# Loads in half-megabyte pieces with two under way, in an expert layer and an attention layer on one core

## The chip, the core and the metric

The kernel runs on one core of a Trainium2 chip. TensorE (PE in the profile) multiplies matrices, VectorE (DVE), ScalarE (ACT) and GpSimd (POOL) work on tiles, and SyncE (SP) issues nearly all transfers. Each engine works through its own list of instructions in order and waits on semaphores for the others. The metric is the time of the device for one execution, in microseconds (us); lower is better.

## The reference

An input of 8 sequences of 512 rows and 256 columns goes through two layers, all in float32. In the first, each sequence picks one of 8 experts by an index; in the second, attention with 16 heads adds a bias that is read from memory for every head, query and key (8 x 16 x 512 x 512 numbers, 134 MB).

```python
def _L0_cond_ref(input_tensor, expert_idx, Wi, bi, Wo, bo, gamma, beta):
    Wi_b = Wi[expert_idx]
    ...
    h = jax.nn.gelu(jnp.einsum('bsh,bhi->bsi', input_tensor, Wi_b) + bi_b[:, None, :], approximate=False)
    o = jnp.einsum('bsi,bih->bsh', h, Wo_b) + bo_b[:, None, :]
    r = o + input_tensor
    ...
    return y * g_b[:, None, :] + be_b[:, None, :]

def _L1_cond_ref(src, src_mask, timestep, attention_bias, W_ada, b_ada, ...):
    emb = jax.nn.silu(_sin_emb(timestep)) @ W_ada + b_ada
    scale, shift = jnp.split(emb[:, None, :], 2, axis=-1)
    x = _ln(src) * (1.0 + scale) + shift
    ...
    scores = jnp.einsum('bhqd,bhkd->bhqk', q / math.sqrt(HEAD_DIM), k)
    scores = scores + attention_bias
    scores = jnp.where(src_mask, -jnp.inf, scores.astype(jnp.float32))
    probs = jax.nn.softmax(scores, axis=-1).astype(v.dtype)
    ctx = jnp.einsum('bhqk,bhkd->bhqd', probs, v)
    ...
    x = x + (ctx @ Wo + bo)
    h = _ln(x) * g2 + beta2
    ff = _gelu2(h @ W1 + b1) @ W2 + b2
    return x + ff
```

## The kernel before, in words

The kernel works through the 8 sequences, called batches here. For each there are an expert layer (`expert_layer`), projections to queries, keys and values (`projections`, `values`), 16 attention steps (`attention_step`, 128 in all, `s` counts them) and a feed-forward layer (`feed_forward`; for the last batch `feed_forward_part`).

*The planner.* None of this is issued in the order in which it is written. Each piece of work is an `op` of the class `Weave`: an engine, a cost in microseconds, a key, the ops that it waits for, the buffers it takes and uses, and a function that emits the instructions. `Weave.run` goes through a modelled time and always emits the op that can start first; among ops that can start within 0.25 us of each other, it takes the one with the lowest key. The keys are in units of attention steps. They come from tables: `PLACES` gives each layer of each batch a start and an end on that scale, `DUE` and `LAST_DUE` shift the parts of an attention step, and `AHEAD` says by how much a load is put ahead of its first user (the last lines of the function). So a change of a table or of a modelled cost gives all five engines another order, with the same work.

*Loads.* `load` makes an op of SP with a cost of the megabytes divided by 0.26. Nearly all loads go by SP's one queue: the bias (`fs`, 1 MB a step, L1085), the masks (`m`, four loads of 32 KB for two steps, L1092), the expert and feed-forward weights (`w`, 1 MB each, L428, L434, L490), the input (`xn`, L422) and its transposed copy (`xt`, L425), 0.5 MB each, the rows of biases and norms (`rows`, L462), and `br`, the first bias of an expert (L439). The outputs leave by it too (L915). As SP is in order, a load that waits for its buffer holds back everything behind it. Every load also has one of eight semaphores in turn, and waits until the one eight before it has landed.

*Buffers.* The bias has five pairs of tiles for two steps each; four steps share two pairs and give them back when the sums over their probabilities are done (L1211). There are two weight buffers, of 1 MB each, one for `rising` and one for `falling` in turn.

*The start.* The index of the experts is loaded by SP (L359), made safe by five small DVE instructions (L368 to L374) and read into a register of SP (`at_expert`, L405). Then `br` of batch 0, its `xt`, another index register and `br` of batch 1, and the first weights in four pieces of 256 KB. On PE the first instruction is the transposition of `br` (L742), and the first weights follow (`up`, L654, then `down`, L677).

*Attention.* Scores begin with a matmul that adds the mask (L1115) and go on with queries times keys (L1122); DVE adds the bias in place and keeps the row maximum (L1135); POOL negates the maximum (L1148); ACT takes the exponential (L1156); DVE transposes (L1171); four steps together are multiplied with the values (L1211), which are 4096 small matmuls of 64x32 in all, and divided. PE runs in three ways of using its array: "dense" 128x128, "scores" 32x64 and "sums" 64x32.

Float32 matmuls run as two passes, so PE has about 27,800 instruction words (weight loads, matmuls and waits). They are fetched from memory while the kernel runs, by the queue that the profile calls q8.

The change touches `load`, the emitting functions of the loads, `expert_layer`, and the tables.

Of the kernel before, what the change touches and what calls it, by code (L numbers as in the profile page):

```python
# [30 lines left out]
def _constants():  # L31
# [13 lines left out]
    for i in range(TURN_PIECES):  # L45
# [13 lines left out]
    "up": [  # L59
        (-30.99, -29.18, 11.93), (-23.38, -4.64, 1.67), (-2.2, -2.19, 2.72), (8.9, 18.36, 0.44),  # L60
        (36.48, 42.61, 6.68), (52.4, 66.61, 8.22), (74.01, 74.43, 3.8), (94.6, 84.17, 0.61),
    ],
    "down": [
        (-28.55, -10.44, -3.1), (3.09, -1.08, -3.11), (8.81, 10.29, 4.11), (14.74, 25.12, -3.62),
        (45.17, 45.46, 12.91), (65.74, 66.53, 0.58), (76.48, 85.13, 4.33), (100.77, 101.12, 0.3),
    ],
    "norm": [
        (-20.56, -11.71, -7.89), (11.44, 22.43, 14.05), (12.2, 41.92, -0.32),
        (21.3, -1.88, -4.88), (15.78, -6.61, -23.47), (31.45, 83.45, -37.13), (93.6, 53.91, -1.4),
        (95.74, 57.42, -8.52),  # L70
    ],
    "project": [
        (-9.61, -7.68, -11.33), (7.41, 20.72, -7.24), (30.64, 30.31, 8.68), (37.76, 54.11, 8.55),
        (49.54, 49.16, 2.1), (80.07, 77.16, 8.86), (97.75, 101.79, 9.6), (104.12, 108.8, -7.13),
    ],
    "values": [
        (0.47, 9.52, 8.56), (20.68, 19.13, 7.24), (38.76, 39.17, 6.29), (52.2, 50.21, -1.61),
        (73.42, 60.72, 3.32), (86.58, 92.54, 11.08), (95.65, 103.53, -1.95),
        (106.56, 111.1, -0.7),
    ],  # L80
    "last_norm": [
        (19.55, 40.44, 3.34), (45.17, 39.05, 0.73), (61.79, 44.12, -1.46), (69.83, 74.12, -1.04),
        (77.81, 88.16, -7.35), (111.66, 102.86, 5.55), (117.29, 111.01, -0.55),
    ],
    "last_up": [
        (30.73, 23.09, -4.57), (46.9, 42.38, 0.97), (68.15, 61.42, 5.34), (86.06, 77.08, 0.85),
        (95.3, 97.21, -3.28), (106.19, 120.06, 3.39), (125.24, 116.66, -2.08),
    ],
    "last_down": [
        (38.56, 21.97, -2.41), (50.89, 52.01, -2.88), (77.89, 66.69, 10.77),  # L90
        (86.82, 82.51, -9.57), (100.48, 114.32, 9.19), (122.04, 112.91, 5.18),
        (124.61, 130.66, 3.47),
    ],
    "last_part": [
        (129.58, 149.24, 3.32), (145.88, 182.54, 3.18), (154.27, 187.28, -2.8),
    ],
}

DUE = {
    "load_m": -0.49, "load_f": 1.05, "convert": -3.58, "add": 1.67, "neg": 0.82, "exp": 0.61,  # L100
    "turn": 5.48, "rec": 9.91, "diagonal": 11.03, "sums0": 2.58, "sums1": 8.57, "sums2": 9.88,
    "sums3": 9.26, "own": 9.45, "spread": 3.43, "divide": 9.16, "out": 6.89, "out_add": 11.41,
}
LAST_DUE = {
    "exp": 1.14, "turn": 8.27, "neg": 6.94, "rec": 7.94, "diagonal": 7.04, "sums0": 2.02,
    "sums1": 5.67, "sums2": 16.43, "sums3": 15.43, "own": 16.77, "spread": 10.61, "divide": 15.33,
    "out": 14.39, "out_add": 30.01,
}

PUT_BACK = {  # L110
    "table": 2.33, "tiles": 0.43,
}

AHEAD = {
    "xt": 2.56, "wi": 1.92, "br": 19.29, "x": -5.59, "wo": 3.7, "row": -0.14, "w1": -3.8,
    "w2": 0.69, "ss": 10.41,
}
# [145 lines left out]
def tile_expert_ffn_then_conditioned_layer(  # L263
# [94 lines left out]
    idx_in = const([1, B], "idx_in", I32)  # L358
    nc.sync.dma_start(idx_in, expert.unsqueeze(0))  # L359
    n_c = 3 + TURN_PIECES  # L360
# [24 lines left out]


    def load(mb, key, emit, **kw):
        return op("SP", mb / 0.26, key, emit, lands=1.8, **kw)

# [29 lines left out]
    for b in range(B):  # L419

        def x_in(b=b):
            nc.sync.dma_start(xn[b].tile, x[b].rearrange("(t p) d -> p t d", p=P))  # L422

        def xt_in(b=b):
            nc.sync.dma_start(xt_h[b].tile, x_t[b])  # L425

        def wi_in(b=b, of=slice(0, FF)):
            nc.sync.dma_start(  # L428
                rising(wi[b])[:, :, of],
                e_wi[at_expert(b)].rearrange("o (c p) f -> p (o c) f", p=P)[:, :, of],  # L430
            )

        def wo_in(b=b):
            nc.sync.dma_start(  # L434
                falling(wo_e[b]), e_wo[at_expert(b)].rearrange("o (c p) d -> p (o c) d", p=P)
            )

        def br_in(b=b):
            nc.sync.dma_start(br[b].tile, e_bi[at_expert(b)].rearrange("o (c p) -> (o c) p", p=P))  # L439

        ld_xt[b] = load_first(b, 0.5, -40, "xt", xt_in, takes=[xt_h[b]])
        if b:
            ld_wi[b] = [load_ahead(1.0, "wi", wi_in, takes=[wi[b]])] * NF
        else:

            ld_wi[b] = []
            for n in range(0, NF, 2):
                def piece_in(n=n, wi_in=wi_in):
                    wi_in(of=slice(n * P, (n + 2) * P))

                o = load(
                    0.25, -39 + 0.01 * n, piece_in, takes=[] if n else [wi[b]],
                    uses=[wi[b]] if n else [],
                )
                ld_wi[b] += [o, o]
        ld_br[b] = load_first(b, 0.02, -39.5, "br", br_in, takes=[br[b]])
        ld_x[b] = load_first(b, 0.5, -37.5, "x", x_in, takes=[xn[b]])
        ld_wo[b] = load_first(b, 1.0, -37, "wo", wo_in, takes=[wo_e[b]])
        ld_rows[b] = []
        for i, v in enumerate((e_bo, e_gamma, e_beta)):  # L460
            def row_in(b=b, i=i, v=v):
                nc.sync.dma_start(  # L462
                    rows[b][i].tile,
                    v[at_expert(b)].rearrange("o d -> (o d)").partition_broadcast(P),
                )

            ld_rows[b].append(load_first(b, 0.3, -36, "row", row_in, takes=[rows[b][i]]))
# [20 lines left out]

    def chunks_in(dst, src):
        return lambda: nc.sync.dma_start(dst, src.rearrange("(c p) n -> p c n", p=P))  # L490

# [25 lines left out]
    for b in range(B):  # L517
        ld_w1[b] = load_ahead(
            1.0, "w1", lambda b=b: chunks_in(rising(w1_h[b]), w1)(), takes=[w1_h[b]]
        )  # L520
        ld_w2[b] = load_ahead(
            1.0, "w2", lambda b=b: chunks_in(falling(w2_h[b]), w2)(), takes=[w2_h[b]]
        )
# [211 lines left out]
    def expert_layer(b):  # L735
# [12 lines left out]
        )  # L748
        first.append((0.2, [(a, 0.0), (e, -1.0)]))
        bias = pool_rows(  # L750
# [3 lines left out]
        def make(f, h, a):  # L754
# [4 lines left out]
                ),  # L759
                deps=[a], uses=[h, bc[b], hid], table="gelu",  # L760
            )

        hids = up(first, lambda: rising(wi[b]), (ld_wi[b], wi[b]), xt, [ld_xt[b], e], hid, make)
        mv = s_mv.new()
# [307 lines left out]
    def attention_step(s):  # L1072
# [11 lines left out]
        def load_f():  # L1084
            nc.sync.dma_start(f(), fside[b, i].rearrange("h q u k -> (h q) u k"))  # L1085

# [201 lines left out]
    for o, what in ahead:  # L1288
        o.key = min(a.key for a in o.after) - AHEAD[what]
    w.run()  # L1290
# [56 lines left out]
```

## Time and profile before

| | |
|---|---|
| runs | 933.25, 933.5, 937.66 us; median 933.5 |
| profiled execution | 933.9 us |
| its span, first to last instruction | 932.1 us |
| granted TensorE clock | 1.000 |
| moved by DMA | 198.08 MB, mean 213 GB/s (191.73 MB read from HBM) |
| first matmul of L654 | at 10.99 us |
| last matmul starts | at 928.4 us |

The time of a run is a little over the span; the span is what the profile divides up. A row of waits gives engine, line, what it waited for, the total in us, the number of times and the longest. A row of the timeline gives start and length in us, engine, line and operation, the output and inputs by the program's names, how many instructions it merges and, in brackets, the idle time before it with what ended it. "SPq" rows are issues of transfers: the time is that of the issue, not of the transfer. The table of DMA issues has, for one transfer from issue to landing, medians of 5.9 us for 1 MB of bias, 3.5 for 0.5 MB of `xt`, 3.3 for 256 KB of `ss` and 3.6 for 32 KB of mask. The trace also holds each packet of each DMA queue with its start, length and size; where the text speaks of packets, they are from there.

### The profile page before, as it was taken

To read this page: it belongs to the slowest core of one execution; us is meant where nothing else is said; L and a number is where in the kernel's file an instruction comes from. 1 tells how busy PE (TensorE), PEld (TensorE's weight loads), DVE (VectorE), ACT (ScalarE), POOL (GpSimd) and SP (SyncE) were. 2 spreads that over 40 slices of the span, in tenths; PEclk is the share of its full clock that TensorE was granted. 3 is DMA by queue.
4 is the path that set the end of the run, shared out by engine and by line. 5 is a ranking of instruction groups with operands and counts; after the bars stand their busy time and mean duration, and the time that the engine had idled before them with its cause. 6 is when DMAs were issued, how large, how long until landed. Compare 5 with 4: busy or idle time off the path is not lost.

```text
span 932.1 us, 33095 instructions
## 1 busy us (share of the span) xinstructions
PE 904.5 (97%) x13841; PEld 531.7 (57%) x13841; DVE 774.7 (83%) x1837; ACT 677.1 (73%) x1452; POOL 297.8 (32%) x380
## 2 busy tenths in 40 slices
PE   5999999999999999999999999999999999999998
PEld 2655564654564574655556546656465555564687
DVE  1226999989999999889999979879889999898951
ACT  2336768758859969589978797595876977959753
POOL 1171636124511435132225322133512632122210
PEclk9999999999999999999999999999999999999999
DMA  7378655676567676557666556754765466567410
GB/s 227 110 245 297 218 207 185 210 253 211 210 225 245 226 280 254 204 208 254 256 223 221 170 195 250 267 191 149 274 240 195 180 249 237 201 228 266 155 59 24
DMA packets 77596, 198.08 MB, mean 213 GB/s; under 512 B 8484, under 2 KB 54902, under 8 KB 61062
## 3 DMA queue, kind: packets, MB, share of 16 engines
q1 hardware_dynamic: 77158, 195.93, 59.3%
q8 instruction: 108, 1.77, 0.8%
q14 instruction: 42, 0.34, 0.1%
q10 hardware_dynamic: 288, 0.04, 0.0%
HBM read 191.73 MB, written 4.21 MB: 210 GB/s over the span
## 4 chain that ended last, share of the span: by engine, by line
PE 66%; DVE 2%; ACT 2%; issue 1%; POOL 0%; DMA 0%; ACTq 0%; DVEq 0%
PE d L677 17%; PE d L654 14%; PE d L1211 11%; PE sc L1122 8%; PE d L825 4%; PE sc L1115 4%; PE d L1254 2%; PE d L873 2%; PE d L1027 2%; PE d L632 1%; PE d L1227 1%; DVE fs L1135 1%; ACT fs L1156 1%; DVE fs L1171 0%; ACT L948 0%
## 5 line engine op out<-in xcount | busy, mean ns | idle before, releaser
L1156 ACT ACTIVATE fs<-fs,top 128x512 f32<-128x512 f32 x512 | 363.5, 713 | 95.1 <-POOL top L1148 93.2
L1135 DVE CUSTOM_DVE_ANT_0 fs<-sc,fs 128x512 f32<-128x512 f32 x512 | 324.0, 682 | 41.4 <-POOL mh L1101 20.4
L1171 DVE STREAM_TRANSPOSE fs<-fs 128x1024 f32<-128x1024 f32 x256 | 304.7, 1218 | 2.2 <-ACT fs L1156 1.9
L677 PE MATMUL d<-w,hid 128*128 128x256 f32 x1024 | 243.2, 386 | 1.7 <-issue 1.4
L654 PE MATMUL d<-xt,w 128*128 128x512 f32 x480 | 223.0, 607 | 4.4 <-DMA w<-in_L_cond_Wi_dram 2.3
L677 PEld LDWEIGHTS d<-w,hid 128*128 128x128 f32 x1024 | 188.0, 190 | 57.7 <-issue 31.8
L654 PEld LDWEIGHTS d<-xt,w 128*128 128x128 f32 x480 | 88.0, 191 | 114.8 <-issue 96.7
L1211 PEld LDWEIGHTS d<-fs,vb 64*32 64x32 f32 x8192 | 113.6, 105 | 60.5 <-issue 47.6
L1211 PE MATMUL d<-fs,vb 64*32 64x128 f32 x8192 | 136.9, 272 | 5.3 <-issue 5.3
L1122 PE MATMUL sc<-k,q 32*64 32x512 f32 x2048 | 136.5, 588 | 1.2 <-issue 1.2
L1101 POOL TENSOR_SCALAR mh<-m 128x512 bf16<-128x512 uint8 x128 | 79.6, 622 | 164.2 <-PE sc L1115 151.7
L1148 POOL TENSOR_SCALAR top<-top 128x4 f32<-128x4 f32 x128 | 25.0, 195 | 288.9 <-DVE top L1135 267.4
L1156 ACT ACTIVATION_READ_ACCUMULATOR fs<-fs,top 128x1 f32 x512 | 96.7, 189 | 0.0
L757 ACT ACTIVATE hid<-d,bc 128x512 f32<-128x512 f32 x64 | 42.8, 687 | 42.9 <-PE d L654 41.8
L727 POOL TENSOR_TENSOR xn<-xn,rows 128x1024 f32<-128x1024 f32 x24 | 56.8, 2365 | 49.4 <-DMA xn<-in_x_dram 21.8
L1156 ACT ACT_TABLE_LOAD x49 | 62.9, 1283 | 0.9
L1115 PE MATMUL sc<-mh,sel 32*64 32x512 bf16 x1024 | 58.3, 398 | 1.6 <-DVE top L1135 0.8
L1115 PEld LDWEIGHTS <-sel 32*64 32x64 bf16 x1024 | 17.3, 101 | 61.0 <-issue 38.9
L1122 PEld LDWEIGHTS sc<-k,q 32*64 32x64 f32 x2048 | 42.8, 130 | 7.0 <-issue 2.1
L695 DVE BATCH_NORM_STATS2 st<-xn 128x6 f32<-128x256 f32 x96 | 40.0, 417 | 7.2 <-POOL xn L727 4.9
L948 ACT ACTIVATE hid<-d,col 128x512 f32<-128x512 f32 x56 | 36.1, 686 | 11.8 <-PE d L654 11.4
L1192 POOL TENSOR_TENSOR dg<-cst,den 128x512 f32<-128x512 f32 x32 | 34.0, 1063 | 33.1 <-DVE den L1187 19.2
(97 smaller groups left out, 730.3 us busy)
## 6 DMA issues: line engine op xcount, KB each, us to landing
fs<-in_fside_Bx16xSxS_dram SPq DMA_DIRECT2D x128, 1024.0 KB, 5.9
w<-in_L_cond_W_dram SPq DMA_DIRECT2D x16, 1024.0 KB, 5.6
w<-in_L_cond_Wo_dram SPq DMA_DIRECT2D x8, 1024.0 KB
m<-in_mask_Bx1xSxS_bk_dram SPq DMA_DIRECT2D x256, 32.0 KB, 3.6
w<-in_L_cond_Wi_dram SPq DMA_DIRECT2D x7, 1024.0 KB, 5.5
xt<-in_x_turned_dram SPq DMA_DIRECT2D x8, 512.0 KB, 3.5
xn<-in_x_dram SPq DMA_DIRECT2D x8, 512.0 KB
out_dram<-xn SPq DMA_DIRECT2D x32, 128.0 KB, 1.7
```

What stands on the lines that cost most here:

```text
L654: nc.tensor.matmul(h.tile, wt[:, c, f * P : (f + 1) * P], src.tile[:, c, :], start=(c == 0), stop=(c == ND - 1),)
L677: nc.tensor.matmul(h.tile[:, :D], lhs(f), wt[:, f, :], start=(f == 0), stop=(f == n - 1))
L695: nc.vector.bn_stats(st, src[:, t, :])
L727: lambda: nc.gpsimd.tensor_tensor(xn[b].tile, xn[b].tile, tiled(row()), alu),
L757: lambda: nc.scalar.activation(hid.tile[:, f, :], h.tile, AF.Gelu, bias=bc[b].tile[:, f : f + 1]),
L1101: nc.gpsimd.tensor_scalar(mh.tile, m8.tile[:, s % 2, :].bitcast(U8), MASKED, 1.0, ALU.mult, ALU.mult)
L1115: nc.tensor.matmul(banks[u][64 * r : 64 * r + 64, :], sel[quads[u]].rearrange("p a q -> p (a q)"), mh.tile[quads[u], :], start=True, stop= ...
L1122: nc.tensor.matmul(banks[u][64 * r : 64 * r + 64, :], q_h[b].tile[quads[u], r, i, :], k_h[b].tile[quads[u], r, :], start=False, stop=True,)
L1135: nc.vector.tensor_tensor_reduce(out=f()[:, u, :], in0=banks[u], in1=f()[:, u, :], scale=1.0, scalar=-3.0e38, op0=ALU.add, op1=ALU.max, ac ...
L1156: nc.scalar.activation(f()[:, u, :], f()[:, u, :], AF.Exp, bias=top.tile[:, u : u + 1], accum_out=den.tile[:, u, s % NI : s % NI + 1],)
L1171: nc.vector.transpose(two, two)
L1211: nc.tensor.matmul(pc[r].tile[QB * u : QB * u + QB, :P], vb_h[b].tile[half, j, u, :], t[half, :, :, u, QB * j : QB * j + QB], start=(j == ...
```

## The change

- `load` counts at least 0.45 us for a load.
- `piece` issues a load on SP and keeps a list of all such loads. From the 17th on, each waits until the one two before it has landed. `in_pieces` cuts a destination along its first free dimension and issues each part with `piece`. The 1 MB loads of bias and weights go in two pieces; `xt`, `xn` and the first weights, which were smaller already, go as one piece each. Masks, rows, `br` and outputs are issued as before.
- The index is loaded from ACT's queue (ahead of the constants), so that SP's first instruction is the load of `xt`. The register of batch 0's index is read by an op of its own (`known`) and the first weights follow it; `br` of batch 0 has a later key.
- In `expert_layer` the transposition of `br` goes behind two tiles of the first layer for batch 0, and stays at the front for the others; GELU waits for it now, not the matmuls.
- Loads that are put ahead have a key of at least −36.
- All tables have other values.

```diff
 PLACES = {
     "up": [
-        (-30.99, -29.18, 11.93), (-23.38, -4.64, 1.67), (-2.2, -2.19, 2.72), (8.9, 18.36, 0.44),
+        (-36.62, -36.27, -8.83), (-13.62, -2.97, 6.75), (4.59, 8.47, 3.94), (13.66, 22.07, 1.07),
...
+UNPACED = 16
...
 AHEAD = {
-    "xt": 2.56, "wi": 1.92, "br": 19.29, "x": -5.59, "wo": 3.7, "row": -0.14, "w1": -3.8,
-    "w2": 0.69, "ss": 10.41,
+    "xt": 5.16, "wi": 11.62, "br": 20.81, "x": 0.62, "wo": 12.39, "row": 18.35, "w1": 7.68,
+    "w2": 7.55, "ss": 1.62,
 }
...
     idx_in = const([1, B], "idx_in", I32)
-    nc.sync.dma_start(idx_in, expert.unsqueeze(0))
+    nc.scalar.dma_start(idx_in, expert.unsqueeze(0))
...
+    sent = []
+
     def load(mb, key, emit, **kw):
-        return op("SP", mb / 0.26, key, emit, lands=1.8, **kw)
+        return op("SP", max(mb / 0.26, 0.45), key, emit, lands=1.8, **kw)
+
+    def piece(dst, src):
+        d = nc.sync.dma_start(dst, src)
+        if len(sent) >= UNPACED:
+            tc.add_manual_dep(
+                d.ins, sent[-2].name,
+                mybir.DependencyInfo(mybir.DependencyClass.Sync, mybir.DependencyReason.DATA),
+                reason="paced",
+            )
+        sent.append(d.ins)
+
+    def in_pieces(dst, src, n):
+
+        step = dst.shape[1] // n
+        for i in range(0, dst.shape[1], step):
+            piece(dst[:, i : i + step], src[:, i : i + step])
...
-        def wi_in(b=b, of=slice(0, FF)):
-            nc.sync.dma_start(
-                rising(wi[b])[:, :, of],
-                e_wi[at_expert(b)].rearrange("o (c p) f -> p (o c) f", p=P)[:, :, of],
-            )
+        def wi_in(b=b):
+            in_pieces(rising(wi[b]), e_wi[at_expert(b)].rearrange("o (c p) f -> p (o c) f", p=P), ND)
...
+            known = op("SP", 1.8, -39.5, lambda: at_expert(0), takes=[wi[b]])
             ld_wi[b] = []
...
                 o = load(
-                    0.25, -39 + 0.01 * n, piece_in, takes=[] if n else [wi[b]],
-                    uses=[wi[b]] if n else [],
+                    0.25, -39 + 0.01 * n, piece_in, deps=[known], uses=[wi[b]]
                 )
                 ld_wi[b] += [o, o]
-        ld_br[b] = load_first(b, 0.02, -39.5, "br", br_in, takes=[br[b]])
+        ld_br[b] = load_first(b, 0.02, -38.97, "br", br_in, takes=[br[b]])
...
-    def chunks_in(dst, src):
-        return lambda: nc.sync.dma_start(dst, src.rearrange("(c p) n -> p c n", p=P))
+    def chunks_in(dst, src, n=1):
+        return lambda: in_pieces(dst, src.rearrange("(c p) n -> p c n", p=P), n)
...
-        first.append((0.2, [(a, 0.0), (e, -1.0)]))
+        turned = (0.2, [(a, 0.0), (e, -1.0)])
...
-                deps=[a], uses=[h, bc[b], hid], table="gelu",
+                deps=[a, e], uses=[h, bc[b], hid], table="gelu",
             )
 
-        hids = up(first, lambda: rising(wi[b]), (ld_wi[b], wi[b]), xt, [ld_xt[b], e], hid, make)
+        hids = up(first, lambda: rising(wi[b]), (ld_wi[b], wi[b]), xt, [ld_xt[b]], hid, make)
+        first.insert(3 if b == 0 else 0, turned)
...
         def load_f():
-            nc.sync.dma_start(f(), fside[b, i].rearrange("h q u k -> (h q) u k"))
+            in_pieces(f(), fside[b, i].rearrange("h q u k -> (h q) u k"), 2)
...
     for o, what in ahead:
-        o.key = min(a.key for a in o.after) - AHEAD[what]
+        o.key = max(min(a.key for a in o.after) - AHEAD[what], -36.0)
     w.run()
```

## The prediction

> **What bounds the kernel now.** I read the page first: the span, the busy row of each engine, the slices and the queues.
>
> ```profile
> span 932.1 us, 33095 instructions
> PE 904.5 (97%) x13841; PEld 531.7 (57%) x13841; DVE 774.7 (83%) x1837; ACT 677.1 (73%) x1452; POOL 297.8 (32%) x380
> PE   5999999999999999999999999999999999999998
> GB/s 227 110 245 297 218 207 185 210 253 211 210 225 245 226 280 254 204 208 254 256 223 221 170 195 250 267 191 149 274 240 195 180 249 237 201 228 266 155 59 24
> q8 instruction: 108, 1.77, 0.8%
> ```
>
> TensorE is busy 97% of the span and idle in one slice only, the first. So a change of the loads can win at the start, in short pauses of PE, and by a better order on PE. Queue q8 matters later: 108 packets of 16 KB. PE's stream in the trace has 27,794 words (a weight load, a matmul or a wait each), which is 108.6 times 256: q8 brings PE its own instructions, 256 words a packet.
>
> Second, what PE waited for, longest first:
>
> ```profile
> PE d L742 <- DMA br<-in_L_cond_bi_dram: 8.4, 1, 8.4
> PE d L1211 <- issue: 5.3, 4, 2.1
> PE d L654 <- DMA w<-in_L_cond_Wi_dram: 2.3, 1, 2.3
> PE d L654 <- ACT hid L757: 1.8, 1, 1.8
> PE d L677 <- issue: 1.4, 1, 1.4
> PE sc L1122 <- issue: 1.2, 1, 1.2
> ```
>
> Two waits on loads stand at the start, and after them none on a load at all; "issue" is PE without anything to wait for. Third, the timeline of the start:
>
> ```profile
> 0.73 0.33 SPq L359 DMA_DIRECT2D idx_in<-in_itok_B_dram  x1
> 3.90 0.35 SPq L439 DMA_DIRECT2D br<-in_L_cond_bi_dram  x1
> 4.29 0.36 SPq L425 DMA_DIRECT2D xt<-in_x_turned_dram  x1
> 6.14 0.42 SPq L428 DMA_DIRECT2D w<-in_L_cond_Wi_dram  x1
> 6.61 0.47 SPq L422 DMA_DIRECT2D xn<-in_x_dram  x1
> 10.99 16.12 PE L654 MATMUL d<-xt,w 128*128 128x512 f32 x32 [2.35 <-DMA w<-in_L_cond_Wi_dram]
> ```
>
> SP sends nothing but the index until 3.90, because its next instruction reads the register that the index fills. Fourth, the timeline round the longest pause:
>
> ```profile
> 526.60 0.41 SPq L434 DMA_DIRECT2D w<-in_L_cond_Wo_dram  x1
> 530.55 1.94 PE L1211 MATMUL d<-fs,vb 64*32 64x128 f32 x116
> 534.64 0.33 PE L1211 MATMUL d<-fs,vb 64*32 64x128 f32 x6 [2.15 <-issue]
> ```
>
> The q8 packet that ends this pause starts at 532.05, as the 1 MB load sent at 526.60 is through, and takes 1.00 us; PE goes on 1.6 us after it. The other long pauses look alike: they stand before word 193 of a packet, and PE resumes about 1.1 us after a packet.
>
> **Where the 932.1 us go.** From start to start PE's steps are constant for each pair of shapes: 429 ns between two 128x512 matmuls, 216 between two 128x256, 518 from scores to anything else, 199 from sums to anything else. Summed over the order of the instructions they give 890.4. Before it stand 8.4 (first transposition), after it 3.8 (last matmul's start to the end). The remaining 29.6 are excess: 2.4 waiting for the first weights; 2.2 in the first five matmuls (0.85 to 0.99 us apart, not 0.43); 11.0 in nine pauses at packet boundaries (0.2 at 120, 1.7 near 194, 0.8 at 225, 1.9 at 373, 0.8 at 445, 2.4 at 532, 2.0 at 687, 0.8 at 719, 0.4 at 794); 14.0 in waits on ACT, DVE and POOL. The "issue" rows (8.7) are smaller than 11.0 because the modelled end of the last matmul covers part of a pause.
>
> **The change, part by part.** *Start.* xt leaves at 0.73, not 4.29, and has landed by 0.73 + 3.55 = 4.3 (its time in the trace: sent 4.29, last engine 7.84). The index goes by ACT's queue at the same 0.73, ahead of the constants and the time steps, which move back by its 0.33; ACT's first work is at 8.93 and the cast of the constants sits behind the index's DVE chain, so that hides. SP reads one index register, not two, before the first weights, which take br's place at 3.90 (before: 6.14). Their landing is bounded by 3.3 us (the median of the 256 KB load ss) and by 4.85 (this load before, with xn interleaved): 7.2 to 8.75. I take 7.6, near the lower end, since only the last of xt is ahead: −3.4 (−2.2 to −3.8). The br transposition now stands behind two weight tiles; its 0.2 to 0.5 us is in the sum of steps below. Later pieces come 0.57 us apart (7.27 to 7.84 for the same pair before) and PE eats one in 3.4 us, so the start carries through.
>
> *Order on PE.* The same matmuls in another order: the steps sum to 888.7, −1.7. Changes between dense, scores and sums fall from 371 to 363, at about 0.1 us each; the rest is which shape precedes them. Bounds −1.7 to 0. The excess that ACT, DVE and POOL cause (14.0) depends on the new places; the new order has the same spacing of score groups (median 5.7 us, lower tenth 4.2 and 4.3), so I leave it at 14.0, with half and one and a half times as ends. One ACT table load fewer (102 to 101) is 1.3 us off the path.
>
> *Pieces.* 128 fs loads and 31 weight loads of 1 MB become halves. DVE gets some 109 more semaphore instructions and ACT some 100; in the trace a met one leaves the gap to the next instruction as it was (−75 ns against −76 on DVE), so nothing, unless the load is late. SP's issues rise by about 0.4 us a piece, and SP is mostly idle waiting.
>
> *Instruction packets.* None of the 108 packets starts before PE is at word 152 of a packet, and PE stops, where it must, before word 193 of the next: it asks near word 155 and has a lead of some 294 words. With under 0.5 MB of loads outstanding at that word the packet starts after a median 1.24 us; with over 1 MB after a mean 3.6 (up to 5.7). It starts mostly as a load ends, so pieces of half the size should halve the 3.6 to 1.8. With 1.0 for the packet and 1.1 until PE resumes, a packet is usable 4.0 us after asking. Against that stands the lead, those words in PE time: sums use 128 words in 0.87 us. In the new order leads are shorter: 26 of 107 are under 5.0 us (15 before), the shortest 2.0 (3.0 before). Adding up what each lead lacks, and letting each pause lengthen the next lead, I get
>
> | usable after asking | 3.3 | 4.0 | 4.5 | 4.8 | 5.3 |
> |---|---|---|---|---|---|
> | old order, us | 0.3 | 1.3 | 2.9 | 4.6 | 11.1 |
> | new order, us | 3.1 | 6.9 | 12.0 | 16.9 | 28.5 |
>
> The old order's 11.0 fixes its delay at 5.3. For the new one I take 4.0, so 6.9: −4.1. The ends are 3.3 (an idle queue) and 5.3 (nothing gained): −7.9 to +17.5. This is the largest term and the least certain.
>
> *The added wait.* From the 17th piece on SP waits until the piece two back has landed. Behind that wait stand masks (POOL's conversion, then scores), index rows, output tiles and further pieces, all in order on SP. Two 0.5 MB loads at 3.5 us each (the xt row) are 300 GB/s; the mean is 213. Counted along PE's order, the median fs load has 17.7 us between the release of its buffer and its use, as before (17.8); the shortest are 3.0 and 4.3. The lower bound is 0; the upper is to stretch the five slices over 262 GB/s (297, 280, 274, 267, 266; 262 is two pieces in 4.0 us) to that rate, 23.3 x (35+18+12+5+4)/262 = 6.6. I take +1.0: before, DVE waited 2.6 us for fs and PE none.
>
> The Trainium skill speaks against this part: "DMA: Bandwidth & Descriptors", section "Rules for kernel authors", asks for at least 1 MiB in a DMA for full bandwidth. Its fit (2.0 us plus bytes at 436 GB/s) makes 3.2 us, or 164 GB/s, of a half-megabyte piece; by that rate, one at a time, the 191.7 MB would take an estimated 1,170 us, while two overlapped reach 328 GB/s and cost nothing.
>
> **Sum.** −3.4 −1.7 −4.1 +1.0 = −8.2, a span of 923.9. The profiled run took 933.9, 1.8 over its span, and the median is 933.5, so 0.4 less: 933.5 − 8.2 = 925.3, say 925.
>
> **The rivals.** *Packets as slow as before.* Two halves under way are still 1 MB in front of a packet. Then the shorter leads pay 28.5: −3.4 −1.7 +17.5 +1.0 = +13.4, 947. For it: the pauses at 373 and 532 stood behind a single 1 MB weight load; against it: waits go by whole loads, and more than 1 MB was outstanding at 39 of 108 askings. It decides where packets become usable later than 4.7 us after asking (pauses over 15.1): then the change loses.
>
> *Late loads take the pauses' place.* The 6.6 instead of 1.0: 925.3 + 5.6 = 931. For it: SP is one queue in order and already waits 198.8 us for mask buffers. Against it: 300 GB/s against 213, and the unchanged slack.
>
> *More than the sum.* Packets behave as with an idle queue (3.1, another −3.8) and the new places halve the 14.0 (−7.0): 914.5. For it: with pieces the queue has shorter spells in front; against it: nothing in the order shows fewer engine waits.
>
> *Only the start works*, with pauses staying at 11: 933.5 − 3.4 − 1.7 + 1.0 = 929. It belongs to the forecast's upper end.
>
> **How the numbers follow.** The forecast (918 to 930) gets 0.52, more than the sum 0.24, late loads 0.14, slow packets 0.10. A measurement tells about 0.5% from no change: under 928.8 is faster, over 938.2 slower. The forecast gives 0.49 of its 0.52 to faster, more than the sum all, late loads 0.04: 0.77. Slower gets 0.07 of the slow packets, whose pauses may also stop between; 0.16 remains for the same. For the range, 914 leaves out about half the upside's lower tail, and 933 leaves out slow packets and the worst late loads: some 0.2 together.
>
> **What would show it.** First L654 matmul between 7.2 and 8.75. "issue" rows of PE under 6 in all; over 12 says slow packets. Packets starting under 2 us after asking where more than 0.5 MB is outstanding. A row of PE or of DVE adds waiting on fs, or POOL on masks, over 5 us says late loads. If PE's waits on ACT, DVE and POOL change by more than 5 us, the places, not the loads, made the time.

## The result and the profile after

The changed kernel took 934.69 us in the median of 20 runs (929.62 to 946.0), the kernel before on the same chip 936.67 (20 runs, 931.74 to 944.59). The ratio is 0.9978, with a 95% interval of 0.9955 to 1.0001. A second comparison (e15 below) gave 0.9994 [0.9968, 1.0020]. So the change makes no difference that can be told here; 925 was forecast, and the range ended at 933. Part of the distance is the base: the forecast started from a median of 933.5 over three runs, 3.2 us under the 936.67 of these 20. The change in time was forecast at −8.2 us, and the medians differ by −2.0. The profiled execution took 934.9 us.

The page of the changed kernel: the span, the engines, the slices of PE and of the data rate, and the queue of the loads (packets, MB, share of the 16 engines' time).

```profile
span 933.0 us, 33576 instructions
...
PE 904.3 (97%) x13841; PEld 533.0 (57%) x13841; DVE 777.0 (83%) x1837; ACT 676.4 (72%) x1451; POOL 297.7 (32%) x380
...
PE   7999999999999999999999999999899999999998
...
GB/s 234 169 224 241 243 253 198 245 205 196 182 249 206 253 230 241 235 223 246 246 200 246 220 208 201 240 211 221 219 235 252 155 225 227 234 212 223 160 63 24
...
q1 hardware_dynamic: 96084, 195.94, 65.6%
```

PE is as busy as before. The first slice has gone from 5 to 7, which is the earlier start; one slice in the middle has gone from 9 to 8, which is new. The loads bring the same bytes at the same rate (212 GB/s, before 213), but their packets take 65.6% of the time of the 16 DMA engines instead of 59.3%.

What PE and SP waited for in the changed kernel (us in total, times, longest). Its lines are about 20 higher than before: L654 is L673, L1211 (sums) L1231, L1115 and L1122 (scores) L1135 and L1142, L1227 L1247.

```profile
PE d L1231 <- issue: 10.5, 10, 2.0
PE d L673 <- DMA w<-in_L_cond_Wi_dram: 7.0, 1, 7.0
PE sc L1135 <- issue: 2.2, 1, 2.2
PE d L1274 <- DVE ctx L1264: 1.2, 1, 1.2
PE d L1247 <- issue: 1.1, 1, 1.1
...
PE sc L1142 <- issue: 0.7, 1, 0.7
...
SPq L395 <- DMA fs<-in_fside_Bx16xSxS_dram: 342.2, 200, 4.1
```

Two things are to be seen. "issue" sums to 14.5 us (10.5 + 2.2 + 1.1 + 0.7) where it was 8.7: PE stands without anything to wait for. And SP waits 342.2 us at the limit of two pieces, yet no row of PE waits on fs, and DVE waits 0.6 us for it: the limit is at work and makes no load late for PE.

The start of the changed kernel, from the timeline:

```profile
0.73 0.52 ACTq L359 DMA_DIRECT2D idx_in<-in_itok_B_dram  x1
0.73 0.39 SPq L395 DMA_DIRECT2D xt<-in_x_turned_dram  x1
...
3.88 1.02 SPq L395 DMA_DIRECT2D w<-in_L_cond_Wi_dram  x2
...
6.98 2.04 PE L673 MATMUL d<-xt,w 128*128 128x512 f32 x2 [6.98 <-DMA w<-in_L_cond_Wi_dram]
```

The start does what it says: the first L673 matmul at 6.98 (6.76 in e15), against 10.99.

Summed from start to start as in the prediction, the two profiled executions part like this:

| us | before | after | change | forecast |
|---|---|---|---|---|
| until PE has its first weights (before: 8.4 + 2.4) | 10.8 | 7.0 | −3.8 | −3.4 |
| PE's steps | 890.4 | 888.7 | −1.7 | −1.7 |
| pauses at packet boundaries | 11.3 | 20.6 | +9.3 | −4.1 |
| waits on ACT, DVE, POOL | 13.6 | 11.1 | −2.5 | 0 |
| late loads | 0 | 0 | 0 | +1.0 |
| slow first matmuls | 2.2 | 1.9 | −0.3 | 0 |
| end | 3.8 | 3.8 | 0 | 0 |
| span | 932.1 | 933.0 | +0.9 | −8.2 |

(Before's pauses are 0.3 larger than in the prediction, by one more small pause that is counted. The waits on engines are what is left of the span; after's 11.1 holds some 1.7 us of a stretch at half clock, which the last section tells of, and before's 13.6 holds none.) These are two single executions. Before's was one of its faster ones, 933.9 us against a median of 936.67, so a span that is 0.9 us longer and a median that is 2.0 us lower go together. In a second profile of the changed kernel (e15 below) the pauses are 18.0 and what is left is 14.3: the growth of the pauses came twice, the fall of the other waits didn't. One pause of the changed kernel, from PE's timeline:

```profile
292.22 2.03 PE L1231 MATMUL d<-fs,vb 64*32 64x128 f32 x128
294.18 0.40 PE L1135 MATMUL sc<-mh,sel 32*64 32x512 bf16 x1
296.76 0.42 PE L1135 MATMUL sc<-mh,sel 32*64 32x512 bf16 x7 [2.18 <-issue]
```

The packet that it waits for was asked for at 289.34, with 0.57 MB of loads in front of it, began at 294.35 and ended at 295.28; PE goes on 1.5 us later. It took 5.0 us to begin, with half a megabyte ahead and a limit of two pieces under way. A lead of 4.8 us (289.34 to 294.18), with its block of sums (128 matmuls in 2 us), was too short.

### The profile page after: what moved, and what is told of

The parts are those of the page before. It is cut to its first block, busy times and chain, and to the rows that moved or that the text cites. A ratio compares the mean times of both kernels' runs of the same rounds, so it can differ in the third digit from the quotient of the medians.

```text
span 933.0 us, 33576 instructions
## 1 busy us (share of the span) xinstructions
PE 904.3 (97%) x13841; PEld 533.0 (57%) x13841; DVE 777.0 (83%) x1837; ACT 676.4 (72%) x1451; POOL 297.7 (32%) x380
## 3 DMA queue, kind: packets, MB, share of 16 engines
q1 hardware_dynamic: 96084, 195.94, 65.6%
## 5 line engine op out<-in xcount | busy, mean ns | idle before, releaser
L696 PE MATMUL d<-w,hid 128*128 128x256 f32 x1024 | 239.5, 385 | 0.1
L673 PE MATMUL d<-xt,w 128*128 128x512 f32 x480 | 224.8, 609 | 7.0 <-DMA w<-in_L_cond_Wi_dram 7.0
L673 PEld LDWEIGHTS d<-xt,w 128*128 128x128 f32 x480 | 87.3, 191 | 121.9 <-issue 100.2
L1231 PEld LDWEIGHTS d<-fs,vb 64*32 64x32 f32 x8192 | 114.2, 105 | 72.2 <-issue 58.6
L1231 PE MATMUL d<-fs,vb 64*32 64x128 f32 x8192 | 140.1, 272 | 10.8 <-issue 10.5
L1142 PE MATMUL sc<-k,q 32*64 32x512 f32 x2048 | 136.8, 590 | 0.7 <-issue 0.7
L1135 PE MATMUL sc<-mh,sel 32*64 32x512 bf16 x1024 | 56.3, 398 | 2.6 <-issue 2.2
L1135 PEld LDWEIGHTS <-sel 32*64 32x64 bf16 x1024 | 16.8, 101 | 58.2 <-issue 41.3
L1142 PEld LDWEIGHTS sc<-k,q 32*64 32x64 f32 x2048 | 42.5, 130 | 7.6 <-issue 2.5
```

Of the source, the lines that this page charges most:

```text
L673: nc.tensor.matmul(h.tile, wt[:, c, f * P : (f + 1) * P], src.tile[:, c, :], start=(c == 0), stop=(c == ND - 1),)
L696: nc.tensor.matmul(h.tile[:, :D], lhs(f), wt[:, f, :], start=(f == 0), stop=(f == n - 1))
L1135: nc.tensor.matmul(banks[u][64 * r : 64 * r + 64, :], sel[quads[u]].rearrange("p a q -> p (a q)"), mh.tile[quads[u], :], start=True, stop= ...
L1142: nc.tensor.matmul(banks[u][64 * r : 64 * r + 64, :], q_h[b].tile[quads[u], r, i, :], k_h[b].tile[quads[u], r, :], start=False, stop=True,)
L1231: nc.tensor.matmul(pc[r].tile[QB * u : QB * u + QB, :P], vb_h[b].tile[half, j, u, :], t[half, :, :, u, QB * j : QB * j + QB], start=(j == ...
```

## The experiments

Each is told as an edit of the changed kernel. "Old tables" are PLACES, DUE, LAST_DUE, PUT_BACK and AHEAD of the kernel before. The measures are those of the prediction. A packet is *asked for* when PE reaches word 155 of the one before; its *lead* is the time that PE's own work takes from there to the word at which PE would have to stop for it. The table gives the leads under 5.0 us among the 107 in PE's order; how long after asking a packet begins, as the mean and as the time that nine in ten keep under (ninth tenth); the pauses at packet boundaries; the span; and the ratio to the kernel before with its interval. All but the ratio are of the one profiled execution.

| kernel | tables, MB per load, limit | leads < 5 | start after asking, mean / 9th tenth | pauses | span | ratio |
|---|---|---|---|---|---|---|
| before | old, 1, none | 15 | 2.65 / 5.07 | 11.3 | 932.1 | 1 |
| changed | new, 0.5, two | 26 | 2.54 / 4.29 | 20.6 | 933.0 | 0.9978 [0.9955, 1.0001] |
| e15 | the same | 26 | 2.47 / 4.08 | 18.0 | 933.3 | 0.9994 [0.9968, 1.0020] |
| e1 | old, 1, none | 15 | 2.78 / 5.38 | 12.6 | 933.3 | 0.9964 [0.9935, 0.9993] |
| e14 | old, 1, two | 15 | 2.72 / 5.11 | 12.7 | 933.4 | 0.9978 [0.9946, 1.0009] |
| e7 | old, 0.5, none | 21 | 2.66 / 4.75 | 9.3 | 925.1 | 0.9918 [0.9889, 0.9947] |
| e2 | old, 0.5, two | 21 | 2.36 / 3.68 | 6.4 | 927.9 | 0.9925 [0.9895, 0.9955] |
| e16 | the same | 21 | 2.40 / 4.12 | 11.2 | 934.4 | 0.9936 [0.9906, 0.9965] |
| e3 | new, 1, none | 21 | 2.85 / 5.45 | 20.8 | 937.2 | 0.9970 [0.9936, 1.0003] |

All but the kernel before have the new start. The short leads don't come from the new tables alone. With loads of 1 MB the old order has 15 and the new one 21 (e3). Halves add five or six to each, because with them PE has some 50 separate waits on semaphores fewer (27,745 words against 27,796 in the new order, 27,746 against 27,794 in the old), and that moves every boundary.

**e1, the start alone.** Old tables, and

```diff
-UNPACED = 16
+UNPACED = 10**9
...
-        step = dst.shape[1] // n
-        for i in range(0, dst.shape[1], step):
-            piece(dst[:, i : i + step], src[:, i : i + step])
+        piece(dst, src)
```

> The change's start alone: order tables of the kernel before, loads of 1 MB, no waits between them. Theory (the start is worth 4.0 us, and the change's other parts give it back at the borders of PE's instruction packets): the first L654 matmul starts at 7.0, the pauses at packet borders stay at 11 us as in the kernel before (a packet is usable 5.3 us after it is asked for, 15 leads under 5.0 us), the span is 928 and the ratio to the kernel before 0.996. Rival (the earlier start is lost again in later waits on ACT, DVE and POOL): the first matmul at 7.0 too, but waits 3 to 4 us longer and a ratio of 0.999 to 1.001.

The first matmul came at 6.77 and the pauses were 12.6, as the theory has it. The ratio is that of the theory as well, but its interval takes in nearly all of the rival's. Its profiled execution has 933.3 for the expected 928: 1.6 of that in pauses, and about 3 in what is left, where two windows at half clock (6.8 us, some 3.4 lost) stand. So the start is worth 3.4 us (0.7 to 6.1) over 12 runs.

**e2 and e16, all but the tables.** Old tables, nothing else.

> All of the change but the order tables: start, halves, two under way, with the tables of the kernel before. Theory: the places decide the leads. By PE's order and the delay that the changed kernel showed (usable 4.9 to 5.0 us after asking) the 21 leads under 5.0 us cost 11 to 12 us, so the span is 890.4 + 7.0 + 3.8 + 1.9 + 12 + 13 = 928, and the ratio 0.996. Rival A (halves and pacing cost time by themselves, whatever the order): pauses of 20 us again, span 936, ratio 1.004. Rival B (pieces do bring packets sooner, at 4.0, and only the new tables spoil it): pauses of 3 us, span 919, ratio 0.986.

> The kernel of e2 once more. Theory: ratio 0.990 to 0.995, 4 us or more below e15, with pauses of 6 to 12 us. Rival (e2 was a lucky sample and the tables make no difference): within 2 us of e15.

**e15, the changed kernel beside e16.** No edit.

> The changed kernel once more, beside e16 on the same chip. Theory: ratio 0.996 to 1.000, pauses of 15 to 25 us in the profiled execution.

The waits of PE in e2 (its L1232 and L1248 are the changed kernel's L1231 and L1247):

```profile
PE d L674 <- DMA w<-in_L_cond_Wi_dram: 6.8, 1, 6.8
PE d L1232 <- issue: 3.0, 4, 1.0
...
PE d L1248 <- issue: 0.6, 1, 0.6
```

"issue" is 3.6 us where the changed kernel has 14.5. With the old tables the same start and the same loads are faster, twice: 929.17 us in e2, and in the direct comparison 931.33 (e16) against 935.88 (e15), 0.5%, with intervals of the ratios that just don't meet. Of e2's expectation neither branch is exact: 6.4 us of pauses lies between the theory's 12 and rival B's 3. In e16 they are 11.2, and the profiled run was that kernel's slowest, so the pauses of a single execution are known to a few us only.

**e3, the new tables with loads as before.** The edit of e1 with the new tables kept.

> The change with its tables and its start, but with loads of 1 MB as before and no waits between them. Theory: pieces leave the mean delay of a packet as it was, so the pauses stay near the changed kernel's 20.6 us: by PE's order 15 us if usable after 5.0, 22 if after 5.3; span 928 to 934, ratio 0.996 to 1.002; packets start a mean 2.5 to 2.7 us after asking. Rival A (pieces and pacing cost): pauses and waits fall by 8 us or more, span 925 or less. Rival B (pieces help the packets much, and without them it would be far worse): pauses of 28 us or more, span 941 or more.

Pauses of 20.8 and packets that begin after 2.85 us: the ratio is the theory's, and the span 3 us over it. Without the pieces the new tables lose as much.

**e7 and e14, halves and limit one at a time.** Old tables; e7 with UNPACED = 10**9, e14 with `piece(dst, src)` in one.

> The kernel of e2 without the waits between loads: halves only, the order on PE the same to the word. If it is the limit of two under way that brings the packets sooner than in e1, the start after asking goes back to a mean of 2.7 us or more and the pauses, by PE's order at 5.3, to 15 to 18 us: span 937 to 940, ratio 1.000 or more. If it is the size of a piece, the mean stays near 2.4 us and the pauses near 6: span 926 to 929, ratio 0.992.

> The kernel of e1 (the change's start, the tables of the kernel before, loads of 1 MB) with the limit of two loads under way: the limit without the pieces. So far a packet started after a mean 2.65 to 2.85 us in every kernel without the limit, halves or not, and 2.28 to 2.54 in every one with it. If the limit is what shortens the delay, the mean is 2.3 to 2.55 here too, the pauses 5 to 9 us by PE's order with 15 leads under 5.0, the span 924 to 929 and the ratio 0.990 to 0.994. If it takes halves and limit together (two loads of 1 MB under way are 2 MB in front of a packet), the mean stays at 2.65 or more and span and ratio are those of e1, 928 to 933 and 0.996.

How soon a packet begins goes by both together: 2.65 to 2.85 us with 1 MB and no limit, 2.72 with the limit alone, 2.66 with halves alone (2.80 in e10), 2.28 to 2.54 in all eight profiled executions with halves and the limit. In time e14 is e1 again, as its second branch says. e7 breaks its first branch: the mean did go back, yet the ratio is e2's. Its pauses are 9.3, not 15 to 18. DVE's waits for the bias show what the limit may cost in return, e2 first, then e7:

```profile
DVE fs L1156 <- DMA fs<-in_fside_Bx16xSxS_dram: 6.2, 9, 1.2
```

```profile
DVE fs L1156 <- DMA fs<-in_fside_Bx16xSxS_dram: 1.4, 2, 1.2
```

With the limit, halves and the old tables DVE waits 6.2 us (9.0 in e16, 6.0 in e9), without the limit 1.4 (2.1 in e10), and what is left of the span beside steps, start, pauses and half clock is 16 to 17 us in e2 and e16 and 13 in e7. So with the old tables the limit seems to lose on late loads some 3 us of what it wins on packets. That rests on few profiles, and nothing was run to test it.

**e4 and e13, hardly any loads.**

```diff
-            in_pieces(f(), fside[b, i].rearrange("h q u k -> (h q) u k"), 2)
+            if s < 10:
+                in_pieces(f(), fside[b, i].rearrange("h q u k -> (h q) u k"), 2)
```

e4 with the new tables, e13 with the old. Both leave out the loads of the bias after step 9 and are there for their time only, two runs each.

> The changed kernel without the loads of the bias (fs) from step 10 on: later steps add what the tile held. PE's order and its instruction words stay. Theory (the packets are slow because loads stand in their way): packets start 1.2 to 1.5 us after asking, usable 3.4 to 3.7, and the pauses fall from 20.6 to 3 to 5 us: span 915 to 918. Rival (the pauses have another cause than the loads, such as PE's own fetching): pauses of 15 us or more, span 928 or more.

> The kernel of e2 (tables of the kernel before) without the loads of the bias from step 10 on; later steps add what the tile held. Beside e4, the same for the new tables (span 916.1, pauses 6.7, waits on engines about 9), it shows what the new tables are worth when packets come quickly. Theory (the new tables are 2 us better in PE's steps and 2 to 4 in waits on engines, and lose it all and more to packets): span 918 to 922 with pauses of 1 to 3. Rival (the new tables are no better than the old even without loads): span 914 to 916.

The waits of PE in e4:

```profile
PE d L673 <- DMA w<-in_L_cond_Wi_dram: 6.8, 1, 6.8
PE d L1232 <- issue: 3.0, 3, 1.3
PE d L845 <- issue: 1.4, 1, 1.4
...
PE sc L1143 <- issue: 0.4, 1, 0.4
```

Packets begin 1.60 us after asking, pauses fall from 20.6 to 6.7, "issue" from 14.5 to 4.8, and the span to 916.1, inside the theory's 915 to 918; the pauses are a little over its 3 to 5. So the loads do hold the packets up. e13 has 1.67, pauses of 4.3 and a span of 919.9, inside its 918 to 922. Between these two profiles the new tables are 3.8 us ahead: 1.7 in steps and 4.8 in what is left (13.0 against 8.2, of which some 1.8 is a window at half clock that only e13 has), less 2.4 in pauses. The medians, 919.95 and 922.14, are 2.2 apart, and the intervals of the ratios overlap (0.9765 to 0.9866 and 0.9789 to 0.9914), so a win of the new tables without loads is not shown. With loads they lose 4.6 in the medians (e15, e16).

**e5, the same work with the packet boundaries elsewhere.** e2, and ahead of the first instruction of PE

```diff
+    warm = const([P, 40], "warm")
+    nc.gpsimd.memset(warm, 0.0)
+    for _ in range(28):
+        nc.tensor.matmul(banks[0][:32, :8], warm[:, :32], warm[:, 32:], start=True, stop=True)
     w.run()
```

> The kernel of e2 (all of the change but the tables) with 28 tiny matmuls on zeros ahead of PE's first work, in the time when it waits for its first weights: 112 words more in PE's stream, so each border of a packet falls 112 words earlier in the same order of work. Theory (a pause is a packet that comes later than its lead): by PE's order the pauses grow from 6.4 us to between 35 (usable after 4.5) and 45 (after 5.0), the span from 927.9 to 955 to 967. Rival (the pauses belong to the loads or to the work at those places, not to the packets' borders): they stay at 6 to 10 us in the same places, span 926 to 932.

The waits of PE in e5:

```profile
PE d L1232 <- issue: 18.2, 11, 2.9
...
PE d L674 <- issue: 2.3, 1, 2.3
...
PE sc L1143 <- issue: 1.8, 1, 1.8
```

The tiny matmuls lie in 1.47 to 4.6 us, before the first weights, and cost nothing there. The span is 954.9, 27.0 over e2's, and the ratio 1.0199 [1.0163, 1.0235]; pauses 30.5 instead of 6.4. The theory's 35 to 45 was too much, the rival's 6 to 10 is out. Nothing of the work or of the loads was changed: the place of the boundaries alone is worth 24 us of pauses. Worked out from PE's order, for boundaries moved by 0 to 248 words and packets usable 5.0 us after asking, the pauses would be 8 to 46 us with these tables and 20 to 55 with the new ones; that is an estimate, of which e5 alone was run.

**e6, e9 and e10, a start that is not slow.** e2 with matmuls on zeros like those of e5: 6 of 512 columns (e6), 4 of 416 with the zeros set by DVE (e9), and e9 without the limit (e10).

> The kernel of e2 with 6 matmuls of 128x512 shape on zeros ahead of PE's first work: PE runs from about 1.5 to 6.8 us, where it waited, and its stream is 24 words longer. If the slow first matmuls (2.7 us over the 0.43 steps in e2) come from PE having stood still, they vanish: -2.0 to -2.7; by PE's order 24 words change the pauses by -0.5 (usable after 4.5) to -4 (after 5.0). Together span 921 to 926 against 927.9, ratio 0.986 to 0.990. Rival (the first matmuls are slow because of the loads that run at the time): the first steps stay at 0.85, span 927 to 928.

> The kernel of e2 (the change with the tables of the kernel before) with 4 matmuls of 416 columns on zeros while PE waits for its first weights, 16 words in all, from about 1 us to 6.5. From e6: the first steps run at 0.43 instead of 0.85 (-2.0 to -2.6), and this time without making the first weights wait. From e5: 16 words more move the borders of the packets a little to the good side, pauses of 4.3 us if usable after 4.5, 8.4 after 5.0. Sum: 6.8 + 890.4 + 5 + 0.3 + 13 to 15 of waits on engines + 3.75, a span of 919 to 922, ratio 0.984 to 0.988. If the warm start is given back at the next wait on ACT, as part of the earlier start was in e1, 922 to 926.

> The kernel of e9 without the waits between loads. Theory from e2 and e7 (mean start after asking 2.36 with the limit, 2.66 without; times within their intervals): the same time as e9 within 0.3%. If the limit of two under way is worth something by itself: e9 ahead by 3 us or more.

PE's timeline at the start, of e6, then of e9:

```profile
1.89 7.20 PE L1314 MATMUL sc<-warm 128*32 128x512 f32 x12 [1.89 <-POOL warm L1312]
9.02 3.70 PE L674 MATMUL d<-xt,w 128*128 128x512 f32 x8
```

```profile
1.35 5.60 PE L1314 MATMUL sc<-warm 128*32 128x416 f32 x8 [1.35 <-DVE warm L367]
6.88 3.70 PE L676 MATMUL d<-xt,w 128*128 128x512 f32 x8
```

Eight steps take 3.70 us here and 6.64 in e2: the slow first matmuls come from PE having stood still. e6 ended too late and held up the first weights by 2.2 us (9.02); e9 didn't. The expected spans still failed: e9's ratio is 0.9903 [0.9870, 0.9936], 2 us under e2's with intervals that overlap, not the 6 hoped for; e6 has 0.9946 [0.9914, 0.9978] and e10 0.9956 [0.9934, 0.9978]. In e9's profile pauses were 11.2; the longest, 3.5 us at 534, stood behind a packet that began 6.5 us after asking. What is won at the start (2.9 us) is less than that one pause. e9 is 5 us ahead of e10, which speaks for the limit; but e2 and e7, the same pair, show nothing of it, so that stays open.

**e8 and e11, quarters.** e2 with four pieces for a bias load, 52 tiny matmuls, and `sent[-4]` (e8) or `sent[-2]` (e11) as the load waited for.

> The kernel of e2 with the bias loads in quarters (256 KB), four pieces under way, and 52 tiny matmuls on zeros at the start (208 words), which put the borders of the packets back to where the leads are long: by PE's order the pauses are 1.4 us if usable after 4.5, 5.7 after 5.0, 10.8 after 5.3. If the size of a piece sets a packet's delay, it falls below e2's (mean 2.36, nine in ten under 3.68) and the span to 922 to 924. If the bytes under way set it, it stays at 2.4 and the span is 923 to 925. If quarters cost the loads their rate, waits on fs appear on PE, or DVE, and the span is over 930.

> The kernel of e8 with two pieces under way instead of four: half a megabyte of bias in front of a packet, not one. If the bytes under way set a packet's delay, its start after asking falls from a mean of 2.35 us to under 1.9 and the pauses from 10.3 to under 5. The price is the rate: if two quarters cannot bring 213 GB/s, PE and DVE get waits on fs of more than 10 us and the span passes 940; otherwise it is 923 to 925.

In e8 a packet begins after 2.35 us, as with halves, pauses are 10.3, and the ratio is 0.9945 [0.9921, 0.9969]: the size of a piece sets nothing, as far as this shows. In e11 it begins after 2.15 and the pauses are 2.4, and it takes 1153.95 us, ratio 1.2311 [1.2261, 1.2360]. What PE and DVE wait for there:

```profile
PE sc L1136 <- DVE top L1156: 88.5, 68, 4.3
PE d L674 <- ACT hid L777: 18.6, 2, 14.0
PE d L674 <- DMA w<-in_L_cond_W_dram: 13.0, 6, 4.5
...
DVE fs L1156 <- DMA fs<-in_fside_Bx16xSxS_dram: 176.3, 104, 9.9
```

The loads come too late to DVE's additions (176.3 us), and PE's scores wait for the DVE behind them (88.5 us); the page gives 172 GB/s over the span where the changed kernel has 212. The rate was the price, as expected, and larger.

**e12, a plan for slower packets.** `TAKES = 8.0` for 4.5 in the planner, new tables. The planner of both kernels counts PE's words and lets an op that needs the next packet start no earlier than `TAKES` us after that packet is asked for (`PACKET, ASKED, NEEDED, TAKES = 256.0, 155.0, 192.0, 4.5` in `Weave`).

> The changed kernel with all its tables, where only the planner's time for a packet is set to 8.0 us instead of 4.5, so that it places the short blocks of sums away from the borders: PE's order sums to 891.9 (+3.5), leads under 5.0 us fall from 26 to 13, and the pauses by that order are 8.6 us (usable after 4.5) to 12.9 (after 5.0). Theory (what the change lost, it lost to short leads): pauses 8 to 13 instead of 20.6, span 924 to 930, ratio 0.988 to 0.993. Rival (the new tables lose by something else): pauses fall and the waits on ACT, DVE and POOL rise by as much, span 932 to 936, ratio 0.997 or more.

PE's waits in e12:

```profile
PE d L1274 <- DVE ctx L1264: 7.7, 6, 3.5
PE sc L1135 <- DVE top L1155: 7.6, 21, 2.0
...
PE d L1231 <- DVE fs L1191: 4.2, 6, 1.4
PE d L1231 <- issue: 4.0, 3, 1.9
```

The pauses are 11.3, as expected, and the span 986.9, ratio 1.0598 [1.0561, 1.0635]: the rival, far beyond its 932 to 936. PE's waits on DVE and ACT grew instead; it looks as if the tables fit one plan only. As a test of the leads it is spoilt, and e13 and e16 took its place.

## Why the prediction was wrong

*The start* was right: −3.8 for −3.4, the first matmul 0.2 us ahead of the lower bound. e1 bears it out (−3.4 in the median ratio).

*Order on PE* was right at −1.7. The 14.0 of waits on engines was less certain than it looked: what is left of the span is 11.1 in the changed kernel, with 1.7 of half clock in it, and 14.3 in e15. I left it at 14.0 because the spacing of score groups was the same. It was the rival *more than the sum* that had the new places lower it, to 7.0; its other half, packets as with an idle queue, did not happen.

*Late loads* cost nothing on PE in the changed kernel, for the +1.0 taken. Halves with two under way carried the same 212 GB/s. The rule of the Trainium skill that was weighed there ("DMA: Bandwidth & Descriptors", section "Rules for kernel authors", at least 1 MiB in a DMA) did not bind at half a megabyte. By the fit of that page, which it gives for DMAs that GpSimd issues, two quarters under way would reach an estimated 202 GB/s; e11, whose loads SP issues, moved 172 on average.

*Instruction packets* is the step that failed, the largest term. It said that a packet "starts mostly as a load ends, so pieces of half the size should halve the 3.6 to 1.8", and with 1.0 for the packet and 1.1 until PE resumes it took a packet as usable 4.0 us after asking. How long a packet took to begin, by the loads that stood in front of it when it was asked for (askings, and their mean in us; a load counts from the end of its issue until its last byte has landed):

| kernel | under 0.5 MB | 0.5 to 1 MB | over 1 MB |
|---|---|---|---|
| before | 59, 1.97 | 12, 2.95 | 37, 3.68 |
| changed | 51, 2.35 | 54, 2.74 | 3, 2.91 |
| e15 | 60, 2.21 | 46, 2.81 | 2, 3.21 |
| e2 | 49, 1.98 | 59, 2.67 | 0 |

The limit did take away the deep queue. But two halves under way mean that half of the packets now have half a megabyte to one in front of them, and those begin after 2.7 us, not 1.8; in all eight executions with halves and the limit that mean is 2.6 to 2.9. The profile before had 12 such askings, with 2.95, so the price stood there to be read. The packets with less in front did not gain either: their median was 1.45 to 2.08 us in those eight, and 1.23 to 1.39 in the six that lack one of the two or both. So the mean over all went from 2.65 to 2.54 only, and of the sign that was named, packets under 2 us where more than 0.5 MB is outstanding, 17 of 57 came. The time until PE resumes was too small as well: in the longer pauses of both kernels PE goes on 1.3 to 1.6 us after the packet's end, 1.6 in the very pause that the prediction shows. 2.5 + 1.0 + 1.5 make 5.0 us after asking, and by the table of the prediction 20.6 us of pauses in the new order stand for 4.9 to 5.0.

The other half of that step, that leads are shorter, was right (26 of 107), though a part of it comes from the halves, as said under the table of experiments. The rival *packets as slow as before* was nearer: it decides over 15.1 us of pauses, and there were 20.6. It did not bring 947, nor a loss, because the delay did fall a little (28.5 would need 5.3) and because no load was late for PE; in the pair of profiles the other waits also fell. I gave it 0.10 against a bet on one number, though the table showed 12 us of pauses at 4.5, which is the planner's own figure, and 16.9 at 4.8. The signal that I had named for it, "issue" over 12 in all, is the one that came: 14.5.

So the expected gain was there in the start and the order, and it was given back at the packet boundaries: in the pair of profiles 9.3 us of pauses against 8.3 won elsewhere (3.8 + 1.7 + 2.5 + 0.3). The version without the new tables keeps a part of it: e16 at 931.33 beats both kernels, and e9 has the lowest ratio of all that do the whole work, 0.9903. Open is why a packet waits 2 us and more behind half a megabyte.

## What to carry to other kernels

When PE is 97% busy and its program is long, its own instruction packets are a load like any other: find the word at which a packet is asked for and the word at which PE stops, and look at what work lies between. A new order has to be judged with the delay that the packets really have, and a few words more or less at the beginning of PE's stream move every boundary (here 24 us for 112 words). Limiting the loads under way takes away the longest queues, but it fills the queue to its limit more often. Before trusting such a limit, look in the profile at hand for the moments when just so much was in front, and read the delay there (here 2.95 us in 12 cases, against the 1.8 taken).

## What the hardware showed

Pauses cost more than their length. The granted clock in the windows after the pause shown above (us from : to, length, busy time and instructions of PE, PEld, DVE, ACT and POOL, clock, DMA share, GB/s):

```profile
294.00:297.50 3.50, 1.32 (x43) 0.49 (x24) 1.43 (x2) 2.55 (x3) 3.26 (x4) 0.99 0.69 209
297.50:300.90 3.40, 3.40 (x34) 1.07 (x20) 2.32 (x8) 1.65 (x3) 0.86 (x2) 0.50 0.39 111
300.90:304.30 3.40, 3.40 (x11) 1.70 (x9) 2.35 (x4) 3.39 (x10) 0.20 (x1) 1.00 0.81 273
```

For 3.41 us PE runs at half speed, just after a window in which it stood for 2.2 of 3.4 us. In the kernels profiled here such drops begin at whole multiples of 3.413 us after the clock was first granted (55 of them, 25 in e11), and last one to four of these windows. 49 follow a window in which PE stood for 1.6 us or more (outside e11 1.8 to 2.9); the most without a drop was 1.95. The other six, as at 207 us in e2, follow one with 0.8 to 1.4 us of standstill. A window at half clock makes PE lose some 1.7 us, beside the pause itself. The Trainium skill has the window ("TensorE: Matmul & The Clock Gate", Part 1: 3413 ns, free-running) and names a whole idle one, about 3.4 us, as what brings the low clock; here well under a whole one was enough.

This goes with much of the spread between executions of one kernel. Over 91 runs of the kernel before, the 30 with a mean clock of 1.000 had a median of 933.6 us, the 31 with 0.998 (one window) 937.4, and the 23 with 0.996 (two) 939.1. The profile that the prediction started from was one of the first kind, and only 3 of the changed kernel's 32 runs were.
